# The odd feature's first operand: from four one-column products to a row of an existing product and a turn on VectorE

## The chip, the cores and the metric

The kernel runs on one core of a Trainium2 chip. The metric is the time of one execution on the device, in microseconds (us). The engines of the core are called by their short names in the profile: PE is TensorE, DVE is VectorE, ACT is ScalarE, POOL is GpSimd, and SP is the engine that issues most of the transfers. "PEld" is TensorE's loading of weights.

## What is computed

The input is x, 64 graphs of 256 nodes with 128 features, in float32, and one 256x256 matrix adj that all graphs share. Four layers follow each other, each with the form x = x + layer(max(layernorm(x), 0)), where the last one gives its result without the sum.

- Layer 0 is a gated recurrent unit over the graph, five steps of it.
- Layer 1 is a two-hop Chebyshev filter; layer 2 is a graph convolution with a normalised result.
- Layer 3 is an attention in which the score of every pair of nodes goes through a leaky ReLU feature by feature, and it is the bulk of the work:

```
s1 = einsum('bkf,ef->bke', x, W1)            # 256 features e for each node
s2 = einsum('bkf,ef->bke', x, W2)
pre = s1[:, :, None, :] + s2[:, None, :, :] + b_lin
h = where(pre >= 0, pre, 0.2 * pre)
e = einsum('bije,e->bij', h, a) + bias
out = sigmoid(einsum('bij,bjf->bif', softmax(e, axis=2), x))
```

In every layer the matrix that is called W or bias here is adj itself, so W1 and W2 are its two halves. For a pair of graphs, `pre` has 2 x 256 x 256 x 256 elements.

## The kernel before

The graphs are taken two at a time, so there are 32 pairs. The work on a pair has three parts.

The **front** of a pair (`front`, L483 to L731) does layers 0 to 2, the normalisation of layer 3 and the operands of the scores: it is a long chain of small products on PE with elementwise steps on ACT, DVE and POOL between them. A 512-column product with 128 features of output is written as four matmuls of 32 output columns each (`side_by_side`, L395), which stand side by side in the array. Transposes by PE (`to_feature`, `to_token`, L414 to L426) use the whole array.

The **tiles** of a pair are 64 slots. The leaky ReLU is split into a linear part and a clipped part. For the clipped part, a slot covers four nodes i of both graphs, and its 256 features lie in two halves on the partitions: a tile of 128 x 2048 elements is min(s1, s2) for one half. DVE makes a tile of the first half of the features with one instruction (L854), ACT makes one of the second half with eight (L868), and POOL makes some of either with eight (L876). In three slots of ten POOL makes the second half and adds it to DVE's tile with a transfer that accumulates (`add_pair`, L893), so that PE reads one tile there and not two. PE weighs the tiles with a by eight passes over 512 columns each (`score`, L935; a float32 matmul is two passes, and each of them has a record in the profile). There are 13 buffers for tiles, named `rl`.

The **tail** of a pair (`tail`, L733) is run once for each 128 of the 256 nodes. It adds the remaining parts to the scores, takes the softmax, weighs the nodes and stores the result.

The signs of a have to be sorted for this, so features with a positive factor stand first. Where the number of positive ones is odd, one feature is left over that belongs with neither half: the **odd feature**. It is not in the tiles. Its share of the score, min(s2o, s1o) with a value per node on each side, is added in the tail by one instruction for each graph (L739), which needs `s1o` with the nodes i on the partitions (128 x 4, for two graphs of two blocks of nodes) and `s2o` as a row of 512 nodes that is the same on all partitions. The linear part `lin` is such a row as well. The two rows come from one small product (L686): the weights `g2` are 32 columns, of which column 0 gives `lin` and column 1 gives `s2o`, and the others are zero. The four quarters of the 512 nodes go to partitions 0, 32, 64 and 96 of the result, ACT copies it to the tile `quarter` (L692), two transfers put rows 0 and 1 of each quarter into a row in memory (L699), and a third one spreads the row over all partitions (L702). The operand `s1o` comes from four more products that alternate with these (L688): here the activations are the weights, 128 x 128, and the moving operand is the single column `w1_odd`. ACT adds the bias and writes `s1o` (L694).

**The order of the work** is fixed when the program is built. A planner in the kernel holds a clock for each engine and a price for each step (`ran`, L106, with PROJECT, MIX, TURN and others, L448). Again and again it gives the engine whose clock stands lowest a step of a chain or a tile, takes the step that is ready, fronts and tails ahead of tiles, paces the front of the pair after next against the tiles that are weighed (`chain_ready`, L960), and gives POOL tiles of the other engines when it is ahead (`part_of`, L818). Every engine then runs its instructions in exactly that order, and each instruction waits for its data only. The planner's prices don't delay anything on the chip: they decide what stands where, and who makes which tile. Banks of PSUM for the front and the tail are taken from a list of three.

Of the kernel before, what the change touches and what calls it, by code (L numbers as in the profile page):

```python
# [8 lines left out]
F32 = mybir.dt.float32  # L9
AF = mybir.ActivationFunctionType  # L10
OP = mybir.AluOpType
# [3 lines left out]
P = 128  # L15
NB = 2
# [6 lines left out]
PE, DVE, ACT, POOL = ENGINES = (mybir.EngineType.PE, mybir.EngineType.DVE, mybir.EngineType.Activation, mybir.EngineType.Pool)  # L23
# [8 lines left out]
def kernel(  # L32
# [50 lines left out]
    nc = tc.nc  # L83
    B, N, D = x.shape
    NC = N // P
# [4 lines left out]
    const = ctx.enter_context(tc.tile_pool(name="const", bufs=1))  # L90
    work = ctx.enter_context(tc.tile_pool(name="work", bufs=2))
# [14 lines left out]
    def ran(engine, us, *after):  # L106
        start = max(clock[engine], 0.0, *after)
        if engine == ACT:
            behind[0] = max(0.0, behind[0] - (start - clock[ACT])) + 0.024 * us
        clock[engine] = start + us  # L110
        return clock[engine] + SEEN[engine] + (behind[0] if engine == ACT else 0.0)
# [6 lines left out]
    spare = [[b, 0.0] for b in banks[5:]]  # L118

    def take():  # L120

        spare.sort(key=lambda b: b[1])
        return spare.pop(0)
# [86 lines left out]
    win_n = const.tile([P, 63], F32, name="win_n")  # L210
    w1 = const.tile([P, N], F32, name="w1")
    w2n = const.tile([P, N], F32, name="w2n")
    odd_one = const.tile([P, 34], F32, name="odd_one")
    g2, w1_odd, b_odd = odd_one[:, 0:32], odd_one[:, 32:33], odd_one[:, 33:34]
    blin_s = const.tile([P, NE], F32, name="blin_s")
    SET_UP = set()

# [44 lines left out]
    def other_constants():  # L262
# [5 lines left out]
        t = ran(DVE, 0.8)  # L268

        for c in range(NC):  # L270
            yield PE, t, 1
            b = take()
            for k in range(NC):
                nc.tensor.matmul(b[0][:, 0:N], adj_t[:, k, c * P:(c + 1) * P], adj_n[:, k, :], start=(k == 0), stop=(k == NC - 1))
            t = ran(PE, 1.2, t, b[1])
            yield DVE, t
            nc.vector.tensor_scalar(adj_2[:, c, :], b[0][:, 0:N], 2.0, None, op0=OP.mult)
            t = ran(DVE, 0.35, t)
# [22 lines left out]
        t = ran(DVE, 1.5)  # L301
        yield PE, t, 1
        b = take()
# [5 lines left out]
        t = ran(PE, 0.6, t, b[1])  # L309
        yield DVE, t  # L310
        nc.vector.tensor_copy(columns(14, 3), b[0][:, 0:3])
        t = ran(DVE, 0.1, t)
# [27 lines left out]
        t = ran(DVE, 1.6)  # L340
# [11 lines left out]
        for c in range(NC):  # L352
            yield PE, t, 1
            b = take()
            for k in range(NE):
                nc.tensor.matmul(b[0][:, 0:N], adj_s[:, k, c * P:(c + 1) * P], moved_to[:, k].rearrange("p h m -> p (h m)"),
                                 start=(k == 0), stop=(k == NE - 1))
            t = ran(PE, 1.2, t, b[1])
# [5 lines left out]
            t = ran(DVE, 0.35, t)  # L364
# [3 lines left out]
        b = take()  # L368
# [8 lines left out]
        t = ran(PE, 1.4, t_in, b[1])  # L377
        yield DVE, t
        nc.vector.tensor_copy(blin_s, b[0][:, 1:4:2])
        nc.vector.tensor_copy(odd_one, b[0][:, 4:38])  # L380
        nc.vector.memset(win, 0.0)
        nc.vector.memset(win_n, 0.0)
        nc.vector.tensor_copy(win[:, 31:32], b[0][:, 0:1])
        nc.vector.tensor_scalar(win_n[:, 31:32], b[0][:, 0:1], -1.0, None, op0=OP.mult)
        t = ran(DVE, 0.7, t)
        spare.append([b[0], t])
        SET_UP.add("all")

# [11 lines left out]
    def flat(t):  # L400
        return t.rearrange("p b n -> p (b n)")
# [43 lines left out]
    SHORT = dict(tag="short", bufs=12)  # L445


    PROJECT, MIX, TURN, PRODUCT, PRODUCTS = 0.86, 1.74, 0.69, 0.88, 2.64  # L448
    COPY, BIASED, TANH, ELEMENTS = 0.48, 0.58, 0.57, 0.61

    def norm(src, since, h):
# [31 lines left out]
    def front(p):  # L483
# [8 lines left out]
        t = yield from norm(x0, 20.0 if p else 3.0, h)  # L492
        yield PE, t, 1
        b = take()
        to_feature(b[0], h)
        t_h = t
        t = ran(PE, TURN, t, b[1])
        yield ACT, t
        hT, t_hT = copied("hT", b, t)
        for step in range(STEPS):  # L500
            yield PE, t_h, 1, lambda: "adj" in SET_UP
            b = take()
            mix_nodes(b[0], h, adj_t)
            t = ran(PE, MIX, t_h, b[1])
            yield ACT, t
            mT, t_m = copied("mT", b, t)
            if p == 0:
# [6 lines left out]
                t = ran(PE, PROJECT, t_m)  # L514
# [3 lines left out]
            else:  # L518
# [4 lines left out]
                t = ran(PE, 2 * PROJECT, t_m, t_hT, pr[1])  # L523
# [3 lines left out]
            t = ran(ACT, TANH, t, r[1])  # L527
# [4 lines left out]
            if p == 0:  # L532
# [5 lines left out]
                t = ran(PE, PROJECT, t_rh)  # L538
            else:
# [7 lines left out]
                t = ran(PE, 2 * PROJECT, t_rh, pv[1])  # L547
# [6 lines left out]
            if p < 1:  # L554
                nc.scalar.activation(pv[0], pv[0], AF.Tanh, bias=bh, scale=1.0)
                t = ran(ACT, TANH, t)
                yield DVE, t
                nc.vector.tensor_sub(d, by_feature(pv[0]), hT)
                t = ran(DVE, ELEMENTS, t)
            else:  # L560
                nc.scalar.activation(d, by_feature(pv[0]), AF.Tanh, bias=bh, scale=1.0)  # L561
                t = ran(ACT, TANH, t)
# [3 lines left out]
                t = ran(POOL, 1.3, t)  # L566
            yield DVE, max(t, t_z)
            nc.vector.scalar_tensor_tensor(by_feature(pr[0]), by_feature(pr[0]), 1.0, d, op0=OP.add, op1=OP.mult)
            t = ran(DVE, ELEMENTS, t, t_z)
# [3 lines left out]
            hT = hT_new  # L573
            t_hT = ran(DVE, ELEMENTS)
# [3 lines left out]
            b = take()  # L578
            to_token(b[0], hT)
            t = ran(PE, TURN, t_hT, b[1])  # L580
# [9 lines left out]
        t = ran(DVE, ELEMENTS, t)  # L590
# [6 lines left out]
        b = take()  # L597
        mix_nodes(b[0], h, adj_n)
        t = ran(PE, MIX, t_h, b[1])
# [3 lines left out]
        b = take()  # L603
        to_feature(b[0], h)
        t = ran(PE, TURN, t_h, b[1])
        yield ACT, t
        hT, t = copied("hT", b, t)
        yield PE, t_h, 1
        b = take()
        mix_nodes(b[0], h, adj_2)  # L610
        t = ran(PE, MIX, t_h, b[1])
# [70 lines left out]
        t_s2a = ran(ACT, COPY, t_s2a)  # L682
        yield PE, t_hT, 1
        b = take()
        for g in range(4):
            nc.tensor.matmul(b[0][g * 32:(g + 1) * 32, 0:P], g2, flat(hT)[:, g * P:(g + 1) * P],  # L686
                             start=True, stop=True, skip_group_check=True)
            nc.tensor.matmul(b[0][:, P + g:P + g + 1], flat(hT)[:, g * P:(g + 1) * P], w1_odd, start=True, stop=True)  # L688
        t = ran(PE, 0.6, t_hT, b[1])
        yield ACT, t  # L690
        quarter = work.tile([P, P], F32, name="quarter", bufs=1)
        nc.scalar.copy(quarter, b[0][:, 0:P])  # L692
        s1o = work.tile([P, NB * NC], F32, name="s1o")
        nc.scalar.activation(s1o, b[0][:, P:P + NB * NC], AF.Identity, bias=b_odd, scale=1.0)  # L694
        t = ran(ACT, 0.35, t)
        spare.append([b[0], t])
        row = dram.tile([2, NB * N], F32, name="row", bufs=2)
        for k in range(2):
            nc.sync.dma_start(row[k].rearrange("(q n) -> q n", q=4), quarter[k:P:32, :])  # L699
            t = moved(t) if k else max(t, moved(t) - 2.2)  # L700
        rows = work.tile([P, 2, NB, N], F32, name="rows")
        nc.sync.dma_start(rows.rearrange("p k b n -> p (k b n)"), row.rearrange("k t -> (k t)").unsqueeze(0).to_broadcast([P, 2 * NB * N]))  # L702
# [352 lines left out]
```

## Time and profile before

| | |
|---|---|
| median of 3 runs | 4951.56 us (4950.31 to 4957.7) |
| time of the profiled execution | 4965.92 us |
| span of the profiled execution | 4964.1 us |
| instructions in the profile | 133991 |
| busy: PE, DVE, ACT, POOL | 4840.3, 4663.4, 4672.1, 4684.9 us |
| tiles: DVE L854, ACT L868, POOL L876 (instructions) | 1813, 10128, 8136 |

The profile is that of one execution, and its time is 14.4 us above the median of the runs. Its span leaves 1.8 us of its time outside. The busy time of PE is an upper figure, because matmuls overlap in its pipeline and their ends are modelled; the distance between the starts of two successive groups of matmuls tells better what one costs. A row of a table of groups gives the line, the engine, the operation, the tiles written and read, their shapes, the count, then the busy time in us and the mean duration in ns, and then the idle time of that engine just before. A row of the table of waits gives who waited for whom, the total in us, how often, and the longest.

### The profile page before, as it was taken

What the parts mean: (1) busy time and instruction counts of PE and PEld (TensorE: products, weight loads), DVE (VectorE), ACT (ScalarE), POOL (GpSimd) and SP (SyncE); (2) the same over time, 40 slices, a digit from 0 to 9 for tenths busy, and PEclk for the clock granted to TensorE, in tenths of its full rate; (3) what the DMA queues carried; (4) which work ended last, traced back from release to release, by engine and by line L of the source; (5) the groups of instructions that cost most, each with busy time, mean ns of one, the idle gap of its engine ahead of it and who ended that gap; (6) DMA issues with size and microseconds to landing.
All of it is one profiled execution on the core that took longest, in us unless ns stands there. A gap on an engine that the chain in (4) does not pass through costs nothing.

```text
span 4964.1 us, 133991 instructions
## 1 busy us (share of the span) xinstructions
PE 4840.3 (98%) x52487; PEld 1793.6 (36%) x52487; DVE 4663.4 (94%) x3288; ACT 4672.1 (94%) x12177; POOL 4684.9 (94%) x9454
## 2 busy tenths in 40 slices
PE   8999999999999999999999999999999999999987
PEld 3333333333333333333333333333333333333322
DVE  3899999999999999999999999999999999999998
ACT  3999999999999999999999999999999999999998
POOL 1899999999999999999999999999999999999998
PEclk9999999999999999999999999999999999999999
DMA  0577667667667676666776676767667767767677
GB/s 18 115 149 145 140 137 148 138 144 150 131 140 147 138 152 138 142 139 135 151 146 139 142 144 132 145 143 144 137 140 145 145 137 143 144 132 144 142 155 145
DMA packets 132363, 687.44 MB, mean 138 GB/s; under 512 B 14096, under 2 KB 49040, under 8 KB 53136
## 3 DMA queue, kind: packets, MB, share of 16 engines
q0 software_dynamic: 88416, 643.86, 64.7%
q1 hardware_dynamic: 42592, 35.01, 2.4%
q8 instruction: 410, 6.72, 0.5%
q14 instruction: 225, 1.84, 0.1%
q10 hardware_dynamic: 720, 0.00, 0.0%
HBM read 26.48 MB, written 8.52 MB: 7 GB/s over the span
## 4 chain that ended last, share of the span: by engine, by line
PE 58%; POOL 11%; DVE 8%; DMA 4%; ACT 4%; issue 3%; POOLq 0%; DVEq 0%; ACTq 0%
PE bank L935 36%; PE bank L398 18%; POOL rl L876 8%; DVE rl L854 6%; DMA rl<-rl 4%; ACT rl L868 3%; PE bank L426 2%; POOL rl L893 1%; PE bank L688 1%; PE bank L686 1%; PE bank L419 1%; POOL d L565 1%; DVE mv L464 0%; POOL mv L393 0%; DVE hT L572 0%
## 5 line engine op out<-in xcount | busy, mean ns | idle before, releaser
L854 DVE TENSOR_TENSOR rl<-s1a,bank 128x2048 f32<-128x2048 f32 x1813 | 4057.4, 2278 | 132.2 <-PE bank L935 70.2
L868 ACT ACTIVATE rl<-bank,s1b 128x256 f32<-128x256 f32 x10128 | 4045.6, 773 | 98.6 <-PE bank L935 57.6
L876 POOL TENSOR_SCALAR rl<-s2n,s1b 128x256 f32<-128x256 f32 x6256 | 2962.8, 669 | 65.0 <-PE bank L935 21.4
L935 PE MATMUL bank<-rl,win_n 128*32 128x512 f32 x17728 | 2198.3, 595 | 56.6 <-DVE rl L854 29.7
L935 PE MATMUL bank<-rl,win 128*32 128x512 f32 x10128 | 1322.4, 594 | 0.0
L935 PEld LDWEIGHTS bank<-rl,win_n 128*32 128x32 f32 x17728 | 555.1, 110 | 1220.6 <-issue 984.5
L876 POOL TENSOR_SCALAR rl<-s2c,s1a 128x256 f32<-128x256 f32 x1880 | 899.2, 658 | 13.6 <-PE bank L935 5.2
L893 POOL DMA_DIRECT2D rl<-rl x614 | 575.6, 949 | 12.5 <-DVE rl L854 6.8
L935 PEld LDWEIGHTS bank<-rl,win 128*32 128x32 f32 x10128 | 324.2, 110 | 653.4 <-issue 535.8
L398 PE MATMUL bank<-mT,wts 128*32 128x512 f32 x2560 | 337.3, 596 | 1.2 <-DVE rh L530 1.1
L398 PE MATMUL bank<-adj_t,h 128*32 128x256 f32 x5120 | 311.8, 383 | 4.8 <-ACT h L584 4.8
L565 POOL TENSOR_TENSOR d<-d,hT 128x512 f32<-128x512 f32 x155 | 227.3, 1466 | 70.0 <-ACT d L561 69.9
L398 PEld LDWEIGHTS bank<-adj_t,h 128*32 128x32 f32 x5120 | 167.8, 111 | 179.2 <-issue 62.1
L468 ACT ACTIVATE h<-x,mv 128x128 f32<-128x128 f32 x384 | 184.2, 766 | 17.3 <-DVE mv L464 16.9
L398 PE MATMUL bank<-hT,wts 128*32 128x512 f32 x1280 | 169.6, 597 | 0.0
L398 PE MATMUL bank<-mT,w 128*32 128x512 f32 x1280 | 168.4, 595 | 0.0
L398 PE MATMUL bank<-rh,u5t 128*32 128x512 f32 x1280 | 167.4, 592 | 0.0
L474 ACT COPY mT<-bank 128x512 f32<-128x512 f32 x160 | 130.4, 815 | 29.9 <-PE bank L398 25.2
L561 ACT ACTIVATE d<-bank,gate_b 128x512 f32<-128x512 f32 x155 | 146.4, 944 | 8.7 <-PE bank L398 8.6
L398 PEld LDWEIGHTS bank<-mT,wts 128*32 128x32 f32 x2560 | 83.5, 110 | 195.5 <-issue 150.8
L526 ACT ACTIVATE bank<-bank,gate_b 128x512 f32<-128x512 f32 x160 | 135.5, 847 | 18.8 <-PE bank L398 18.7
L549 ACT ACTIVATE bank<-bank,gate_b 128x512 f32<-128x512 f32 x160 | 144.2, 901 | 8.8 <-PE bank L398 8.5
(166 smaller groups left out, 3501.6 us busy)
## 6 DMA issues: line engine op xcount, KB each, us to landing
rl<-rl POOLq DMA_DIRECT2D x614, 1024.0 KB, 7.9
rows<-row SPq DMA_DIRECT2D x32, 512.0 KB
xin<-in_x_dram SPq DMA_DIRECT2D x64, 128.0 KB
out_dram<-o SPq DMA_DIRECT2D x64, 128.0 KB
row<-quarter SPq DMA_DIRECT2D x64, 2.0 KB
w_raw<-in_L_gnn_w_w_dram SPq DMA_DIRECT2D x3, 128.0 KB
th_raw<-in_L_gnn_Theta_dram SPq DMA_DIRECT2D x1, 320.0 KB
adj_n<-in_adj_dram SPq DMA_DIRECT2D x1, 256.0 KB
```

The source lines that it names most:

```text
L398: nc.tensor.matmul(o[g:g + 32], w[:, g:g + 32], t, start=start, stop=stop, skip_group_check=True)
L468: nc.scalar.activation(h[:, k, :], s[:, k, :], AF.Relu, bias=mv[:, k, 0:1], scale=mv[:, k, 1:2])
L474: nc.scalar.copy(c, by_feature(bank[0]))
L526: nc.scalar.activation(r[0], pr[0], AF.Tanh, bias=br, scale=0.5)
L549: nc.scalar.activation(pr[0], pr[0], AF.Tanh, bias=bz, scale=0.5)
L561: nc.scalar.activation(d, by_feature(pv[0]), AF.Tanh, bias=bh, scale=1.0)
L565: nc.gpsimd.tensor_sub(d, d, hT)
L854: nc.vector.tensor_tensor(t, rows.to_broadcast(whole), ops["s2a"].unsqueeze(1).to_broadcast(whole), op=OP.min)
L868: nc.scalar.activation(t[:, g, b, :], s2p[:, b, :], AF.Relu, bias=ops["s1"][1][:, b, i:i + 1], scale=-1.0)
L876: nc.gpsimd.tensor_scalar(t[:, part, b, :], ops["s2n" if k else "s2c"][:, b, :], ops["s1"][min(k, 1)][:, b, row], MOST_NEGATIVE, op0=OP.mi ...
L893: nc.gpsimd.dma_start(out=t.rearrange("p g b n -> p (g b n)"), in_=z.rearrange("p g b n -> p (g b n)"), accum_op=OP.add)
L935: nc.tensor.matmul(pe[g * 32:(g + 1) * 32, :], w[:, 31 - r:63 - r], flat(t[:, g]), start=False, stop=(left[block] == 0), skip_group_check= ...
```

## The change

The four one-column products and ACT's instruction on them are gone. Column 2 of the weights `g2`, which was zero, now holds the weights of the odd feature's first operand, so that row 2 of each quarter of the existing product is s1o without its bias, and nothing more is multiplied. To have it with the nodes on the partitions, DVE transposes the 128x128 tile `quarter` in its blocks of 32x32, and takes column 2 of each block, with the bias added, as `s1o`. For that to come out in the right places, the moving operand of matmul g is no longer the g-th quarter of the nodes, but the g-th 32 nodes of each block of 128; it is read with a stride. The two transfers of the rows put the nodes back in order: each moves 4 x 4 pieces of 32 elements, where it moved 4 pieces of 128. Two prices of the planner are changed with it and one is new, and so is one price that belongs to another step: TURN, for four transposes on PE.

```diff
-    odd_one = const.tile([P, 34], F32, name="odd_one")
-    g2, w1_odd, b_odd = odd_one[:, 0:32], odd_one[:, 32:33], odd_one[:, 33:34]
+    odd_one = const.tile([P, 33], F32, name="odd_one")
+    g2, b_odd = odd_one[:, 0:32], odd_one[:, 32:33]
...
-        nc.vector.tensor_copy(odd_one, b[0][:, 4:38])
+        nc.vector.tensor_copy(odd_one[:, 0:32], b[0][:, 4:36])
+        nc.vector.tensor_copy(odd_one[:, 2:3], b[0][:, 36:37])
+        nc.vector.tensor_copy(b_odd, b[0][:, 37:38])
...
-        t = ran(DVE, 0.7, t)
+        t = ran(DVE, 0.9, t)
...
-    PROJECT, MIX, TURN, PRODUCT, PRODUCTS = 0.86, 1.74, 0.69, 0.88, 2.64
+    PROJECT, MIX, TURN, PRODUCT, PRODUCTS = 0.86, 1.74, 0.80, 0.88, 2.64
...
+        tokens = flat(hT).rearrange("p (q g i) -> p q g i", g=4, i=32)
         for g in range(4):
-            nc.tensor.matmul(b[0][g * 32:(g + 1) * 32, 0:P], g2, flat(hT)[:, g * P:(g + 1) * P],
-                             start=True, stop=True, skip_group_check=True)
-            nc.tensor.matmul(b[0][:, P + g:P + g + 1], flat(hT)[:, g * P:(g + 1) * P], w1_odd, start=True, stop=True)
-        t = ran(PE, 0.6, t_hT, b[1])
+            nc.tensor.matmul(b[0][g * 32:(g + 1) * 32, 0:P], g2, tokens[:, :, g, :], start=True, stop=True, skip_group_check=True)
+        t = ran(PE, 0.35, t_hT, b[1])
         yield ACT, t
         quarter = work.tile([P, P], F32, name="quarter", bufs=1)
         nc.scalar.copy(quarter, b[0][:, 0:P])
+        t = ran(ACT, 0.3, t)
+        spare.append([b[0], t])
+        yield DVE, t
+        turned = work.tile([P, P], F32, name="turned", bufs=1)
+        nc.vector.transpose(turned, quarter)
         s1o = work.tile([P, NB * NC], F32, name="s1o")
-        nc.scalar.activation(s1o, b[0][:, P:P + NB * NC], AF.Identity, bias=b_odd, scale=1.0)
-        t = ran(ACT, 0.35, t)
-        spare.append([b[0], t])
+        nc.vector.tensor_scalar(s1o, turned[:, 2:P:32], b_odd, None, op0=OP.add)
+        ran(DVE, 0.4, t)
         row = dram.tile([2, NB * N], F32, name="row", bufs=2)
         for k in range(2):
-            nc.sync.dma_start(row[k].rearrange("(q n) -> q n", q=4), quarter[k:P:32, :])
+            nc.sync.dma_start(row[k].rearrange("(q g i) -> g q i", g=4, i=32), quarter[k:P:32, :].rearrange("g (q i) -> g q i", i=32))
```

Lines of the changed kernel stand 2 further on from L383 on and 5 further on after this place, so L854 becomes L859, L868 becomes L873, L876 becomes L881 and L935 becomes L940. The new matmuls are L689, the transpose L698 and the addition L700.

## The prediction

> **What bounds the kernel now.** I read the busy shares on the page first, then stretches of the span, then PE's timeline around the lines that change, then the waits.
>
> ```profile
> PE 4840.3 (98%) x52487; PEld 1793.6 (36%) x52487; DVE 4663.4 (94%) x3288; ACT 4672.1 (94%) x12177; POOL 4684.9 (94%) x9454
> ```
>
> Four engines stand close together, so the average decides nothing. Busy time by stretch (length, then PE, PEld, DVE, ACT, POOL) says more:
>
> ```profile
> 0.00:134.90 134.90, 111.94 (x1103) 49.75 (x1107) 42.77 (x116) 46.60 (x82) 14.84 (x26) 0.87 0.07 18
> 134.90:4940.00 4805.10, 4716.97 (x51300) 1740.12 (x51294) 4615.73 (x3165) 4623.21 (x12090) 4669.22 (x9427) 1.00 0.70 142
> 4940.00:4964.10 24.10, 11.35 (x95) 3.71 (x94) 4.86 (x8) 2.30 (x6) 0.88 (x1) 0.71 0.40 82
> ```
> ```profile
> 2000.00:3000.00 1000.00, 988.86 (x10796) 365.00 (x10792) 956.46 (x665) 956.54 (x2495) 974.76 (x1967) 1.00 0.69 142
> ...
> 4800.00:4940.00 140.00, 118.55 (x1062) 33.61 (x1058) 138.81 (x71) 139.94 (x383) 139.37 (x291) 0.99 0.78 159
> ```
>
> The first tile starts at 134.9, and the last 24 us are one pair's tail. Between them, with fronts in the mix, PE is 99% busy while DVE and ACT idle 4% and POOL 2.5%. After the last front (4800 on) it is the reverse: PE 85%, the others above 99%. So the three elementwise engines can run full when PE has room, and in the steady stretch they don't.
>
> PE's timeline over one occurrence of the changed lines:
>
> ```profile
> 2501.53 1.04 PE L935 MATMUL bank<-rl,win_n 128*32 128x512 f32 x8
> 2502.38 0.38 PE L686 MATMUL bank<-hT,odd_one 128*32 128x128 f32 x2
> 2502.70 0.38 PE L688 MATMUL bank<-odd_one,hT 128*128 128x1 f32 x2
> 2503.01 0.41 PE L686 MATMUL bank<-hT,odd_one 128*32 128x128 f32 x2
> ...
> 2504.64 0.38 PE L688 MATMUL bank<-odd_one,hT 128*128 128x1 f32 x2
> 2504.95 1.06 PE L935 MATMUL bank<-rl,win 128*32 128x512 f32 x8
> ```
>
> From 2502.38 to 2504.95 is 2.57 us, back to back, while eight 512-column passes of L935 take 0.85. The narrow products and the full-array ones alternate, so neither kind overlaps with itself. The same distance is 2.57 us in 31 of the 32 fronts and 4.32 in the first, at half clock: 84.0 us in all.
>
> Waits in 500 to 4500 us (total, times, longest):
>
> ```profile
> DVE rl L854 <- PE bank L935: 58.7, 97, 2.0
> ACT rl L868 <- PE bank L935: 51.7, 71, 2.7
> ...
> DVE rl L854 <- DMA rl<-rl: 35.2, 27, 3.7
> ACT rl L868 <- DMA rl<-rl: 31.1, 22, 3.4
> ...
> POOL rl L876 <- PE bank L935: 22.7, 27, 2.4
> ```
>
> The largest waits of all three are for tile buffers that PE hasn't weighed yet. PE paces the steady stretch, though by little.
>
> **What the Trainium skill says.** "TensorEngine Tiling (Array Packing)", section Key Properties: different column tiles can load and multiply in parallel, while a change of tiling mode drains TensorE. The trace agrees: four 32-column matmuls with 128 moving columns (th_raw and w,yT rows) start four in 109 ns, but each of the eight parts here takes 0.31 to 0.33 us. "Perfetto Trace Analysis", section Identifying the Most-Contended Engine, says that matmul busy time is no good measure for TensorE; so I count distances between starts. "VectorE: DVE Perf Modes", section The three transpose paths, prices VectorE's transpose of 128x128 at 311 ns in bf16, in 32x32 blocks; no run here shows it.
>
> **The change part by part.**
>
> *PE.* 84.0 us go. In come four side-by-side matmuls of two passes, 2 x 0.109 = 0.22 us per front, 7 us in 32. The net is 77 us: 2.35 in each later front, about 3.9 in the first (4.32 less twice 0.22). The strided moving operand has no precedent in the trace. Its runs are 32 contiguous elements; nothing to gain from it, and if it halved the rate, 0.22 us per front, 7 us in all. I take no extra.
>
> *ACT.* 32 instructions of L694 go, 10.9 us. The planner gives it 24 fewer tile instructions (10104), at 4045.6/10128 = 0.40 us: 9.6. Together 20.5 less.
>
> *DVE.* 32 transposes and 32 additions on 128x4 come. For the transpose the nearest rows are elementwise instructions on 128x128 (L297, 285 ns); with the skill's 311, I take 0.30, with 0.28 and 0.55 (if four bytes halve the rate) as ends. For the addition, 0.17 (L258, 128x2), at most 0.37 (L464, 128x4). That is 0.47 us per pair, 15 us (14 to 29). It also gets 4 more tiles (1817) at 4057.4/1813 = 2.24: 9.0. Together 24 more. The copies at set-up (two more, 0.16 each) lie before 134.9, where DVE is two thirds idle; without that cover, 0.3 us.
>
> *POOL.* 8 fewer instructions (8128) at 0.475: 3.8 less.
>
> *Waits.* The transpose waits for ACT's copy of `quarter`; behind it in DVE's queue stand tile instructions (L854 before, L859 now) or the step L568, for whom PE waits. The addition waits for the transpose, a few tenths inside the 0.47. The bank comes free an ACT instruction (0.34) sooner. s1o and the rows are used 90 us later (first rows issued 133.2, first L739 at 223.5), so neither DVE's step nor slower landing of shorter pieces reaches anything: 64 transfers, 0.5 us each on SP; were issue twice as long, 32 us on an SP that has 240 transfers in the whole span. Without the 90 us it would be the landing, which the trace doesn't give; up to a microsecond or two per pair.
>
> *The planner.* Its price of the odd step was 0.6 where 2.57 was spent. Four transposes cost about 0.70 (in PE's timeline the passes begun at 2489.74 last to 2490.60, and the group after the transposes starts at 2491.30); their price goes from 0.69 to 0.80, ten times per pair. Per pair the plan was 2 us short on PE; now it's some 1 us over. No price delays anything; it moves the order towards PE being early, which should cut waits, but I count nothing for it.
>
> **The sum**, on the profiled execution. Start: 134.9 - 3.9 = 131.0. End: 24.1. The middle is the longest of:
>
> - PE: 30 of its fronts' steps lie in the stretch that PE paces (234.8 to 4628.8; the last is at 4781.7): 4805.1 - 30 x 2.35 = 4734.6. Span 4889.7.
> - POOL: 4669.2 - 3.8 = 4665.4 busy, 54 us of short gaps between its instructions (under 0.1 us each), and longer waits, now 82. In the table above those for PE and the accumulating transfers (15.9) are 38.6 of 71.5, so 44 of the 82; I let PE's share (26) go and two thirds of the transfers' (18): 44 stay. Middle 4763, span 4918.
> - DVE: 4615.7 + 24 = 4639.7 busy, waits now 189. For PE (58.7 + 13.4 on the tail's reciprocal) they're 44%, for the transfers 21%; with the same cuts 80 stay, and 5 new: middle 4725, span 4880.
> - ACT: 4623.2 - 20.5 = 4602.7 and even all of its 182: 4785. With the same cuts below DVE.
>
> So POOL becomes the bound, at 4918; with 1.8 outside the span 4920 against 4965.9, 46 us less. The same 46 off the median of 4951.56 gives **4906 us**.
>
> **The rivals.**
>
> *All of it comes through.* PE keeps the pace with as little slack as now, and POOL's waits shrink with it. For it: POOL's short waits may largely be PE's delay passed through the transfers; in 4800 to 4940 it was busy 99.5%. Against it: at a middle of 4735, POOL would have 16 us for all its long waits. Span 4890: median 4877.
>
> *Little comes through.* The order is new from the first pairs on, and the three engines' waits for each other (DVE for POOL's L393 and L565, POOL for DVE, the transfers) stay as they are. If half of POOL's 26 for PE goes and nothing else, 69 of its 82 stay: middle 4788, span 4944, 20 less; median 4931.
>
> *Slower: DVE's queue behind the new wait.* One instruction on DVE now waits for ACT in every front, and ACT already runs late at times (DVE L530 waited for ACT 25.8 us in 13 cases, the longest 6.9). While DVE stands, tiles of 2.24 us each stand behind it and PE runs dry. DVE's busy and its waits that aren't PE's make 4639.7 + 106 = 4746 in the middle; it passes the old 4805 once the new wait averages above (4805 + 4 - 4746)/32 = 2.0 us. At 3 us the middle is 4842, the span 4997, the median 4984. Against it: the planner puts the transpose after the copy by its clock, and behind one to three tile instructions that cover lateness.
>
> *It doesn't shorten PE's step:* the strided operand makes the four run one after another. At 0.27 us per pass (L686's alone takes that long), eight take 2.2 us and 0.4 of 2.57 is saved, 13 us of PE in all, with DVE's 24 us in its idle time: at most 13 us, median near 4942.
>
> **How the numbers follow.** A measurement of this kernel tells about 0.2% (9.9 us) from no change. The likeliest case, 4890 to 4925: 0.57. All comes through, 4865 to 4890: 0.14. Little comes through, 4925 to 4941: 0.14. Within 0.2%, the serial matmuls or a new order that eats the rest: 0.06. Slower: 0.09. So faster 0.85. The range of 8 in 10 goes from 4872 to 4943; it leaves about 0.05 below and 0.15 above, and DVE's upper bound (14 us more) and the stride's 7 lie within it.
>
> **What would show it.** In the profile after: matmuls on `quarter`'s bank from 0.2 to 0.3 us apart from the next group, not 2.57; the first tile near 131; transposes near 0.3 us; DVE's and ACT's waits for PE's L940 well below 58.7 and 51.7 in the same stretch; POOL's share of the middle above 98%; PE's below 98.5%. It is wrong if the transpose waits above 2 us on average, if PE stays at 99% with a shorter step (then something else fills it), or if POOL's long waits don't fall.

## The result and the profile after

The changed kernel takes 4942.76 us (median of 20 runs), the kernel before 4952.4 us in 20 runs: a ratio of 0.9978, 95% interval 0.9971 to 0.9984. It is faster by some 10 us. The forecast was 46 us faster, 4906; the direction was right and the size was not. The profile after shows a run at its kernel's median. The profile of before stands 14 us above its own; the first experiment tells why.

The changed step itself became what the sum made of it. PE's timeline of the changed kernel (start, time to the modelled end, engine, line) around one occurrence:

```profile
2485.62 0.40 PE L689 MATMUL bank<-hT,odd_one 128*32 128x128 f32 x8
2485.84 1.04 PE L940 MATMUL bank<-rl,win 128*32 128x512 f32 x8
```

The next group starts 0.22 us later. Summed over the 32 fronts the distances are 7.2 us, where they were 84.0: PE's 77 us are gone, and the strided operand costs nothing that can be seen (eight passes start within 0.22 us, as the sum had it). The span of the profiled execution is 4940.7 us (its time is 4942.5), and the busy line and two stretches (as before: length, then PE, PEld, DVE, ACT, POOL) read:

```profile
PE 4758.5 (96%) x52231; PEld 1739.0 (35%) x52231; DVE 4682.1 (95%) x3358; ACT 4644.4 (94%) x12121; POOL 4659.6 (94%) x9446
```
```profile
2000.00:3000.00 1000.00, 977.43 (x10764) 355.28 (x10756) 964.01 (x678) 960.09 (x2512) 968.67 (x1962) 1.00 0.69 141
...
4800.00:4920.00 120.00, 97.85 (x911) 28.71 (x907) 117.79 (x61) 120.00 (x331) 117.03 (x243) 0.99 0.80 161
```

PE is down from 989 to 977 in that thousand, and DVE, ACT and POOL stand at 96 to 97% as they did. So PE got room, and no other engine filled up. The waits in 500 to 4500 us of the changed kernel say what they wait for now:

```profile
PEld bank L428 <- DVE hT L574: 108.0, 79, 3.2
ACT rl L873 <- DMA rl<-rl: 66.0, 39, 5.2
...
DVE rl L859 <- DMA rl<-rl: 57.1, 50, 3.5
...
PE bank L428 <- DVE hT L574: 48.4, 54, 2.6
...
ACT rl L873 <- PE bank L940: 44.4, 50, 4.1
...
POOL rl L881 <- DMA rl<-rl: 26.7, 26, 2.5
...
DVE rl L859 <- PE bank L940: 13.0, 30, 2.1
...
POOL rl L881 <- PE bank L940: 7.9, 11, 2.2
```

DVE's and POOL's waits for PE fell from 58.7 to 13.0 and from 22.7 to 7.9, as forecast; ACT's hardly did (51.7 to 44.4). But the waits for the accumulating transfers, which the sum let fall by two thirds, rose: for DVE from 35.2 to 57.1, for ACT from 31.1 to 66.0, for POOL from 15.9 to 26.7. And PE, early now, stands before its transposes until DVE has made hT: 156 us (PE and its weight loads) where it was 75. Two theories could account for a gain of 10 us instead of 46. **A**: the gain was lost in the new order of the instructions, which the planner's changed prices made. **B**: behind PE there was at once another bound, whatever the order.

### The profile page after: what moved, and what is told of

Read it like the earlier page. It is cut to its first block, busy times and chain, and to the rows that moved or that the text cites. A ratio compares the mean times of both kernels' runs of the same rounds, so it can differ in the third digit from the quotient of the medians.

```text
span 4940.7 us, 133662 instructions
## 1 busy us (share of the span) xinstructions
PE 4758.5 (96%) x52231; PEld 1739.0 (35%) x52231; DVE 4682.1 (95%) x3358; ACT 4644.4 (94%) x12121; POOL 4659.6 (94%) x9446
## 5 line engine op out<-in xcount | busy, mean ns | idle before, releaser
L873 ACT ACTIVATE rl<-bank,s1b 128x256 f32<-128x256 f32 x10104 | 4050.2, 793 | 128.9 <-DMA rl<-rl 70.9
L859 DVE TENSOR_TENSOR rl<-s1a,bank 128x2048 f32<-128x2048 f32 x1817 | 4064.8, 2280 | 90.4 <-DMA rl<-rl 62.7
L881 POOL TENSOR_SCALAR rl<-s2n,s1b 128x256 f32<-128x256 f32 x6280 | 2951.1, 656 | 64.2 <-DMA rl<-rl 28.2
L940 PE MATMUL bank<-rl,win_n 128*32 128x512 f32 x17752 | 2191.5, 594 | 57.1 <-DVE rl L859 28.9
L940 PE MATMUL bank<-rl,win 128*32 128x512 f32 x10104 | 1316.5, 594 | 0.0
L940 PEld LDWEIGHTS bank<-rl,win_n 128*32 128x32 f32 x17752 | 559.4, 110 | 1216.5 <-issue 992.8
L881 POOL TENSOR_SCALAR rl<-s2c,s1a 128x256 f32<-128x256 f32 x1848 | 872.7, 637 | 5.9 <-DMA rl<-rl 1.2
L940 PEld LDWEIGHTS bank<-rl,win 128*32 128x32 f32 x10104 | 323.1, 110 | 641.4 <-issue 533.1
L428 PE MATMUL bank<-ident,hT 128*128 128x128 f32 x640 | 105.4, 288 | 69.2 <-DVE hT L574 61.7
L528 ACT ACTIVATE bank<-bank,gate_b 128x512 f32<-128x512 f32 x160 | 144.3, 902 | 20.5 <-PE bank L400 16.5
L551 ACT ACTIVATE bank<-bank,gate_b 128x512 f32<-128x512 f32 x160 | 151.4, 946 | 11.3 <-PE bank L400 11.3
## 6 DMA issues: line engine op xcount, KB each, us to landing
rl<-rl POOLq DMA_DIRECT2D x614, 1024.0 KB, 7.9
```

The costliest lines, as they stand in the source:

```text
L528: nc.scalar.activation(r[0], pr[0], AF.Tanh, bias=br, scale=0.5)
L551: nc.scalar.activation(pr[0], pr[0], AF.Tanh, bias=bz, scale=0.5)
L859: nc.vector.tensor_tensor(t, rows.to_broadcast(whole), ops["s2a"].unsqueeze(1).to_broadcast(whole), op=OP.min)
L873: nc.scalar.activation(t[:, g, b, :], s2p[:, b, :], AF.Relu, bias=ops["s1"][1][:, b, i:i + 1], scale=-1.0)
L881: nc.gpsimd.tensor_scalar(t[:, part, b, :], ops["s2n" if k else "s2c"][:, b, :], ops["s1"][min(k, 1)][:, b, row], MOST_NEGATIVE, op0=OP.mi ...
L940: nc.tensor.matmul(pe[g * 32:(g + 1) * 32, :], w[:, 31 - r:63 - r], flat(t[:, g]), start=False, stop=(left[block] == 0), skip_group_check= ...
```

## The experiments

Each run is told as its ratio to the kernel before on the same chip, since the level of that kernel differed between occasions: its median was 4952 to 4955 us on three chips and in the 20 runs above, and 4965 and 4967 us on two other chips. A gain in us in what follows is the ratio's distance from 1, times 4952.

### The same order, only PE's step shortened

```diff
-            nc.tensor.matmul(b[0][:, P + g:P + g + 1], flat(hT)[:, g * P:(g + 1) * P], w1_odd, start=True, stop=True)
...
-        nc.scalar.activation(s1o, b[0][:, P:P + NB * NC], AF.Identity, bias=b_odd, scale=1.0)
+        nc.scalar.activation(s1o, b[0][:, 0:NB * NC], AF.Identity, bias=b_odd, scale=1.0)
```

> The kernel before with only the four one-column products (L688) taken out; s1o is then made from other columns of the same bank, so the odd feature's part of the score is not the reference's. The planner's prices are as before, and every engine's order of instructions is that of before. PE's step shrinks from 2.57 to 0.22 us per front and DVE gets nothing. Theory A, the gain was lost in the new order: 4900 to 4917, since PE's freed time comes through where the order is the old one. Theory B, PE was only just ahead of the next bound, which is the engines' waits for each other and for the accumulating transfers whatever the order: 4932 to 4945, with the waits of DVE, ACT and POOL for PE falling and those for transfers rising by about as much.

Measured: 0.9939 (0.9926 to 0.9952), 30 us. That is between the two theories' figures, so each holds a part: even in the old order only two fifths of the 77 us come through, and the whole change brought a third of these 30. Its waits in 500 to 4500 us:

```profile
PEld bank L426 <- DVE hT L572: 92.1, 71, 3.2
...
DVE rl L853 <- DMA rl<-rl: 49.5, 39, 3.1
...
ACT rl L867 <- PE bank L934: 44.3, 59, 3.0
...
ACT rl L867 <- DMA rl<-rl: 34.5, 27, 3.5
...
DVE rl L853 <- PE bank L934: 28.1, 50, 2.2
...
POOL rl L875 <- DMA rl<-rl: 17.9, 21, 2.6
...
POOL rl L875 <- PE bank L934: 9.1, 8, 2.4
```

With the order untouched, the waits for PE fall and those for transfers don't: over the four engines these are 138 us, where they were 103. They aren't PE's lateness passed on, or they would have fallen with it.

The busy line of this run, and its middle from the first tile to the last tail (length, then PE, PEld, DVE, ACT, POOL), can be set beside the prediction's sum for POOL:

```profile
PE 4769.6 (97%) x52231; PEld 1746.9 (36%) x52231; DVE 4654.2 (95%) x3288; ACT 4665.8 (95%) x12177; POOL 4664.9 (95%) x9454
```
```profile
133.10:4897.70 4764.60, 4649.71 (x51058) 1695.35 (x51054) 4606.73 (x3165) 4617.32 (x12090) 4649.15 (x9427) 1.00 0.70 143
```

POOL has the same 9454 instructions in the same order as in the profile of before, and they take 20 us less, 4664.9 instead of 4684.9. That is the occasion, not the edit. Where POOL's tile instructions follow each other directly, one starts 451 ns after the other in the profile of before and 449 ns here. For tiles of whole width it is 451 in every profile from the two chips with the level of 4965 and 4967, and 449 in every other one. So the profile from which the sum was made belongs, by POOL's pace, to the slower kind of occasion, and the medians of the result to the faster. With a level that is 11 to 12 us higher on the chips of the slower pace, that accounts for most of the 14 us between them.

POOL is idle for 115 us of this middle. Gaps under 0.1 us make 54 of them, as the sum took it. The longer waits were 82 us and are 62; the sum let them fall to 44. An estimate for the occasion of the profile of before: 0.9939 of its span is 4934 us, and with this run's start and end, POOL's 4669 us of that occasion and 54 of short gaps, 55 us of longer waits are left, give or take 6.

### The whole change in the old order

The changed kernel with the planner's prices of before, and DVE's two instructions not charged.

> The whole change, but with the planner's prices of before (TURN 0.69, odd step 0.6, nothing charged for DVE's two new instructions, which stand in DVE's order where ACT's step was planned). All other instructions stand in the order of before. Theory A: 4903 to 4922, well below the changed kernel's 4943. Theory B: 4935 to 4950, the same as the changed kernel within 0.2%. A third outcome, above 4952, would say that the two instructions on DVE cost their price and more, through waits for ACT's copy.

Measured: 0.9967 (0.9954 to 0.9979). That is in theory B's range, 0.0028 above the run before it, 14 us. The two runs differ in DVE's two instructions, which stand where nobody planned them: they take 1.56 us per front from the transpose to the next instruction, and 0.89 in the changed kernel, where the plan has them; and the transpose made DVE wait for ACT's copy 11 times, 12.7 us in all. They also differ in ACT's instruction that is gone and in the shorter pieces of the row transfers. That DVE's part makes the 14 us is likely and not shown.

### TURN by itself

```diff
-    PROJECT, MIX, TURN, PRODUCT, PRODUCTS = 0.86, 1.74, 0.80, 0.88, 2.64
+    PROJECT, MIX, TURN, PRODUCT, PRODUCTS = 0.86, 1.74, 0.69, 0.88, 2.64
```

> The changed kernel with TURN at 0.69 instead of 0.80, nothing else; a new order results. Theory A in the form that the overcharge of TURN spoils the order: 4905 to 4928. Theory B: 4935 to 4950. If orders are a lottery of some 10 to 20 us whatever the prices, anything from 4925 to 4960, with PE idle in the same places as in the changed kernel.

> The kernel before with TURN at 0.80 and nothing else changed. Theory A (the price of TURN makes a worse order): 4965 to 4990. Theory B: 4945 to 4962, no change that can be measured, since PE is full in either order.

> The changed kernel with TURN at 0.74, between 0.69 (0.9954 of before) and 0.80 (0.9978); 0.60 gave 1.0003. If the price acts by itself: 0.995 to 0.998, and PE's waits for ACT's h between 62 and 103 us. If orders are drawn by chance: anywhere in 0.992 to 1.002.

> The changed kernel with TURN at 0.60, below what four transposes cost (0.70). With 0.80 ACT's copy of h came 1.06 us after the transposes on average and PE waited 103 us for h in 500 to 4500 us, with 0.69 0.87 and 62. If a price above the cost is what does harm, since ACT is given one more piece of a tile before the copy: 0.994 to 0.997 of before, as with 0.69. If lower is better still: below 0.994. If prices only draw another order out of many: anywhere in 0.993 to 1.000, and waits for h not in step with the price.

Measured: the change with 0.69 gives 0.9954 (0.9943 to 0.9966); the kernel before with 0.80 gives 1.0033 (1.0021 to 1.0045); the change with 0.74 gives 0.9972 (0.9962 to 0.9983), with 0.60 it gives 1.0003 (0.9994 to 1.0011). The first of these lies just above theory A's range, the second within it. So the new price costs 0.0024 in the changed kernel and 0.0033 in the kernel before, 12 and 16 us, though nothing waits for a price. In both, PE's waits for ACT's tiles h grew by the same amount: 59 to 101 us in the kernel before, 62 to 103 in the changed one (500 to 4500 us). In these pairs ACT's copy of hT after the transposes also starts later, 1.65 us after them on average instead of 1.35 in the kernel before, 1.70 instead of 1.29 in the changed one. That fits a plan which takes the transposes to end later and gives ACT a piece of a tile first, which no run shows by itself. But neither the waits nor the time follow the price. At 0.74 the waits for h are 110 us, longer than at 0.80, while the ratio lies between those of 0.69 and 0.80. At 0.60 they are shortest (47 us) and the time is worst; there PE waits 75 us for transfers and 88 for DVE's tiles. So the 12 and 16 us are what two pairs of orders differ by, and not a cost per unit of the price; that any price would draw a better or a worse order by chance isn't ruled out.

### DVE's new addition

The changed kernel's own rows show that the addition of four columns is dear (what the expectations call the port is the idea that DVE and POOL share a way into SBUF; the last section comes back to it):

```profile
L698 DVE STREAM_TRANSPOSE turned<-quarter x32: 289/306/314, 127.3 to 4755.8; 128x128 f32<-128x128 f32 x32
L700 DVE TENSOR_SCALAR s1o<-turned,odd_one x32: 229/392/2326, 127.7 to 4756.2; 128x4 f32<-128x4 f32 x32
```

The three numbers are the shortest, median and longest duration in ns. The edit takes it out, and ACT adds the bias in its copy:

```diff
-        nc.scalar.copy(quarter, b[0][:, 0:P])
+        nc.scalar.activation(quarter, b[0][:, 0:P], AF.Identity, bias=b_rows, scale=1.0)
...
-        nc.vector.tensor_scalar(s1o, turned[:, 2:P:32], b_odd, None, op0=OP.add)
+        s1o = turned[:, 2:P:32]
```

> The changed kernel without DVE's addition: the bias goes into ACT's copy of the product (a bias per partition that is zero outside rows 2, 34, 66 and 98), and the tail reads the turned tile. Every other instruction stands where the changed kernel has it. Theory of the port: DVE's addition takes 0.23 us where POOL is idle and up to 2.3 us where POOL's instructions stand close[...]; without it DVE gains 0.55 us per front on average, 18 us in all, and 5 to 10 us of them come through: 4932 to 4939. Rival: the addition's waits fall into time in which DVE would have waited anyway: 4940 to 4946.

> The same removal of the addition in the kernel with TURN at 0.69, where the addition took 0.99 us on average (to 4.3), so 32 us of DVE. Theory of the port: 10 to 20 us faster than with the addition, 4912 to 4922. Rival: 4928 to 4934, no change.

Measured: 0.9983 (0.9977 to 0.9989) beside the changed kernel's 0.9978, and 0.9947 (0.9935 to 0.9959) beside 0.9954. The first is its rival's figure; the second lies between its two expectations, and its interval covers no change. So nothing that could be measured changed in either. The addition's long durations are real, and taking them out brings no time. With the share of DVE's time that comes through in the next experiment (0.13), 18 us would have brought 2 to 3 us, which these intervals can't tell from nothing.

### How much of each engine's time comes through

In these the orders are those of before, and one engine's tiles are a little narrower, for instance POOL's:

```diff
+CUT = 8
...
-                nc.gpsimd.tensor_scalar(t[:, part, b, :], ops["s2n" if k else "s2c"][:, b, :], ops["s1"][min(k, 1)][:, b, row],
+                nc.gpsimd.tensor_scalar(t[:, part, b, 0:N - CUT], ops["s2n" if k else "s2c"][:, b, 0:N - CUT], ops["s1"][min(k, 1)][:, b, row],
```

> The kernel before, every engine's order unchanged, with POOL's tile instructions 248 columns wide instead of 256 (8 of every 256 columns of its tiles are left out). That takes some 11 ns from each of 8136, about 90 us from POOL's busy time. Theory C, the four engines are coupled and none of them alone sets the pace: a fifth to a third comes through, 4925 to 4936, like the 28 us that came of PE's 77. Theory D, POOL was the bound behind PE: over half, below 4908.

> The kernel before, orders unchanged, with DVE's tile instructions 250 columns wide instead of 256 (6 of every 256 columns of its tiles are left out): [...]50 ns from each of 1813, about 90 us of DVE. Theory C: 4925 to 4940. Theory D in the form that DVE is the bound behind PE, since PE waited longest for DVE's hT in the changed kernel: below 4908.

> The kernel before, orders unchanged, with ACT's tile instructions 244 columns wide instead of 256 (12 of every 256 columns of its tiles are left out), some 8 ns from each of 10128, about 85 us of ACT. Taken from PE, POOL and DVE in the same order, 77, 52 and 84 us of busy time brought 28 to 30, 26 to 28 and 11 us: shares of 0.38, 0.5 and 0.13, which already make up 1. Theory C, the pace is shared and the shares add to one: ACT's share is near nothing, 0 to 10 us faster than before. Rival: the shares don't add up to anything and ACT brings 20 us or more as well.

> The kernel before, orders unchanged, with the four one-column products taken out (the odd feature's part of the score is then not the reference's) and POOL's tile instructions 248 columns wide (8 of every 256 columns of its tiles are left out). Alone these brought about 0.6% and 0.5%. If the engines hold each other up in turn, the two together bring at least their sum: 0.985 to 0.989 of before. If POOL becomes the bound once PE is relieved, as the prediction had it, more than the sum: below 0.985. If a third bound stands close behind both (DVE, ACT, the transfers), less: above 0.991.

The busy lines of the three with one engine cut (POOL, DVE, ACT) show by how much:

```profile
PE 4838.3 (98%) x52487; PEld 1792.9 (36%) x52487; DVE 4662.3 (94%) x3288; ACT 4671.2 (94%) x12177; POOL 4632.8 (94%) x9467
```
```profile
PE 4841.2 (98%) x52487; PEld 1797.4 (36%) x52487; DVE 4579.3 (92%) x3288; ACT 4671.1 (94%) x12177; POOL 4685.2 (95%) x9467
```
```profile
PE 4836.7 (98%) x52487; PEld 1792.9 (36%) x52487; DVE 4662.2 (94%) x3288; ACT 4576.2 (92%) x12177; POOL 4665.5 (94%) x9467
```

| taken from | us taken | ratio | us gained | share |
|---|---|---|---|---|
| PE | 77 | 0.9939 (0.9926 to 0.9952) | 30 | 0.39 |
| POOL | 52 | 0.9947 (0.9935 to 0.9959) | 26 | 0.50 |
| DVE | 84 | 0.9978 (0.9970 to 0.9987) | 11 | 0.13 |
| ACT | 88 to 96 | 0.9993 (0.9986 to 0.9999) | 3 | 0.04 |
| PE and POOL | 77 and 53 | 0.9847 (0.9834 to 0.9861) | 76 | |

What was taken is counted between profiles with the same pace of POOL: the first two lines above are from a chip where POOL's tile instructions of whole width start 451 ns apart, as in the profile of before. The third, like the run with PE and POOL cut, is from one with 449; its POOL has 4665.5 us although only ACT's work was cut. (In two other profiles from that chip ACT's tile instructions start 357.0 ns apart instead of 357.8; hence the range in its row.)

POOL's cut was smaller than expected (6 to 7 ns from each instruction, not 11), and its share, a half, lies between those of the two theories. Together PE and POOL bring more than their sum of 56: once PE is relieved, POOL's 53 us bring 46, with an interval of some 9 us to either side. So POOL is close behind PE, as the prediction's sum had it; the run's figure itself stands on the border between the two expectations of at least the sum and more than the sum. DVE and ACT hardly matter. That the four shares add to about 1 is no rule, since PE's and POOL's don't add up when both are cut.

### The accumulating transfers

```diff
-        nc.gpsimd.dma_start(out=t.rearrange("p g b n -> p (g b n)"), in_=z.rearrange("p g b n -> p (g b n)"), accum_op=OP.add)
+        nc.gpsimd.dma_start(out=t[:, 0:2].rearrange("p g b n -> p (g b n)"), in_=z[:, 0:2].rearrange("p g b n -> p (g b n)"), accum_op=OP.add)
```

> The kernel before, orders unchanged, with each accumulating transfer moving half of the tile (the other half of POOL's part is left out of the sum). The transfers land some 2 to 3 us sooner than 7.9. If waits for the transfers are a bound of their own behind PE (they were 31 to 66 us per engine in the changed kernel), 15 to 40 us faster than before. Theory C without the transfers: up to 10 us faster.

> The changed kernel with accumulating transfers of half the size (half of POOL's part is left out of the sum), orders unchanged. In the kernel before the same cut brought 46 us. Theory L: PE's freed time is waiting behind the transfers, so here the cut brings clearly more than 46 us from the changed kernel's 0.9978, to 0.980 to 0.986 of before. Rival, it brings the same 46 or less, since the changed order loses elsewhere (PE's waits for ACT's h): 0.987 to 0.992.

The transfers of the first of these (size, and median us from issue to landing), where the kernel before has 1024.0 KB and 7.9:

```profile
rl<-rl POOLq DMA_DIRECT2D x614, 512.0 KB, 4.8
```

Measured: 0.9906 (0.9892 to 0.9919) in the kernel before, 46 us with no engine's work cut, more than either theory had, and 0.9866 (0.9853 to 0.9879) in the changed one, 55 us from its 0.9978. In both the waits of DVE, ACT and POOL for transfers go to under 4 us each, and PE's to nothing. So the time to the transfers' landing was a bound beside PE in the kernel before already, at 98% busy PE. The second result lies between the figures of its two theories, and the difference of 9 us between the two gains isn't clear of noise: that the change made the transfers a heavier bound isn't shown, and most of the 55 us was there before.

### The plan's price of a landing

The planner takes a transfer to land 6.6 us after the end of its issue. In the traces it is 6.9 (median), and over 10.7 in one of twenty. So some buffers and tiles are planned for moments at which they aren't there.

```diff
-ISSUE, ADDED, LANDED, SLACK = 0.65, 5.3, 6.6, 0.3
+ISSUE, ADDED, LANDED, SLACK = 0.65, 5.3, 7.9, 0.3
```

> The changed kernel with TURN at 0.69 and the planner's price for the landing of an accumulating transfer raised from 6.6 to 7.9 us; it really takes 6.9 (median) from the end of the issue, 10.7 for one in twenty. A new order results. Theory L, what holds the kernel back with PE relieved is that PE and the tile buffers wait for transfers that the plan expects too early: 0.988 to 0.993 of before, and waits for transfers below those with 6.6. Rival: an order as good or bad as any other, 0.994 to 1.000.

> The kernel before with the landing price at 7.9 instead of 6.6 and nothing else. If the better price of a landing is what brought 31 of the 42 us of the run with TURN at 0.69, and PE didn't bound the kernel before: 0.990 to 0.995 of before. If PE's 77 us more of work keep the kernel before from using it: 0.996 to 1.001.

> The changed kernel as it is, TURN at 0.80, with the landing price at 7.9. If waits for transfers are what took the gain and the plan's price of them sets these waits, 0.990 to 0.9945 of before, with waits for transfers in 500 to 4500 us below 80 us over the four engines (168 in the changed kernel). If TURN's effect stays beside it: 0.002 or more above the run with TURN at 0.69 (0.9915). If the 0.9915 was the luck of one order: 0.995 to 1.000.

| program | landing 6.6 | landing 7.9 |
|---|---|---|
| before | 1 | 0.9965 (0.9951 to 0.9979) |
| changed, TURN 0.80 | 0.9978 (0.9971 to 0.9984) | 0.9933 (0.9920 to 0.9945) |
| changed, TURN 0.69 | 0.9954 (0.9943 to 0.9966) | 0.9915 (0.9902 to 0.9927) |

The waits for transfers in the last of these, 500 to 4500 us:

```profile
POOL rl L881 <- DMA rl<-rl: 12.8, 7, 4.5
...
ACT rl L873 <- DMA rl<-rl: 10.4, 7, 2.2
...
DVE rl L859 <- DMA rl<-rl: 8.9, 6, 3.0
```

The table is nearly additive. In each row the landing price brings 0.0035 to 0.0045, and the waits for transfers over the four engines fall from 103 to 21, from 168 to 41 and from 111 to 43 us. That is a new order in each case too, but three pairs of orders agree. For the kernel before, the figure falls among those of its second expectation, that PE's extra work keeps it from using the better price; but the changed kernel gains no more, so that isn't the reason. In each column the change with TURN at 0.69 brings 0.0046 to 0.0050, and TURN at 0.80 takes 0.0018 to 0.0024 of it back (at 7.9 the two intervals overlap). At the price of 7.9 the waits for h are the same at both TURNs (44 and 45 us), so what TURN costs there, if anything, is not those waits, and stays open. The kernel with TURN 0.69 and landing 7.9, 4910 us, beats both kernels of this study by more than the change did.

### Fewer joined slots

> The changed kernel with TURN at 0.69 and 28 slots in a hundred joined by a transfer instead of 30: some 41 tiles go from POOL to ACT, with 41 transfers of 614 fewer, and PE weighs 41 tiles more (35 us). Theory: PE has room now, POOL and the transfers have not, ACT has: 0.988 to 0.993 of before. Rival: PE is still the bound and the order is another: 0.996 to 1.003.

Measured: 0.9973 (0.9962 to 0.9984), with an interval that overlaps that of the same kernel with 30 in a hundred (0.9954). The edit didn't do what the expectation says. The transfers went from 614 to 573 and PE weighs 41 tiles more, but the planner gave the work back to POOL: its tile instructions rose from 8112 to 8192 (ten tiles of eight), ACT's fell from 10064 to 10056, and DVE made 9 tiles fewer. So this run says nothing on taking work from POOL.

## Why the prediction was right or wrong

**PE's step, and that the stride costs nothing:** right, 2.57 to 0.22 us.

**DVE's 0.47 us per front, ends 14 and 29 us in all:** the transpose was right (0.31). The two together took 0.89 us per front, 28 us: the value taken was wrong, and the upper bound held in this order, though not in the one with TURN at 0.69 (42 us) or the old one (50 us). That DVE has the time for it was right in the sense that removing the addition brings nothing. The whole of DVE's new step with the order that comes with it, TURN aside, is the difference between 0.9939 and 0.9954, 7 us where the sum had none; the two intervals overlap.

**The step that failed first: POOL's waits.** "I let PE's share (26) go and two thirds of the transfers' (18): 44 stay." With only PE's step shortened and every order as before, 62 of the 82 us stay (by the estimate, 55 in the occasion of the profile), so 20 to 27 us of waits go where the sum took 38. In 500 to 4500 us, 9.1 of POOL's 22.7 us for PE stay, and its 15.9 for the transfers become 17.9. Those waits have a cause beside PE's lateness, as the half-size transfers and the landing price show. PE's relief is worth 30 us and not 46. Of these 16 us some 11 are the waits, by the same estimate; 4 are the eight instructions of POOL that only the new plan takes from it, and 2 are the first tile, which came at 133.1 us and not at 131.0 (in the changed kernel it comes at 131.2). In the changed kernel the waits for transfers rose from 103 to 168 us over the four engines. POOL's longer waits are 89 us there and its share of the middle is 97.0%, where the prediction named more than 98% and a fall of these waits as its signs.

**"So POOL becomes the bound, at 4918":** POOL's time then comes through almost in full, so that it stands next is right, with the transfers beside it. The span is right by luck: 4920.3 was profiled with only PE's step shortened, but in a faster occasion. There POOL is busy for 4649 us of the middle where the sum has 4665, and idle for 115 where it has 98 (54 and 44), and the two differences cancel. "The same 46 off the median" was a fair step; what it took off was too much.

**"No price delays anything ... I count nothing for it": wrong.** The first half is true. But the order that TURN 0.80 makes costs 12 us in the changed kernel and 16 in the kernel before.

So of the forecast 46 us, 16 are lost in what PE's relief brings, POOL's waits above all, 7 in DVE's step and its order, and 12 by TURN, which leaves 11, and 10 was measured. These are the steps from one run to the next, so they add up by themselves; a different way through the runs would give each another size. Of the rivals, "little comes through" is nearest. It kept the waits for transfers, and left 69 of POOL's 82 us; 62 were measured in the old order. It had neither the 7 us nor TURN's 12. DVE's queue behind the transpose, the slower rival, didn't come: in the changed kernel the transpose made DVE wait once, 5.7 us in the first front.

## What to carry to other kernels

In a kernel with several engines near 95%, a busy share can't tell who sets the pace: shorten one engine at a time by a per cent with the order fixed, and see what share comes through. Here it was 0.39 of PE's time, 0.50 of POOL's, 0.13 of DVE's and next to nothing of ACT's, and the time to a transfer's landing weighed as much as PE did: half-size transfers brought 46 us.

Before two spans are compared, look at one instruction that the edit doesn't touch. Here POOL's same instructions took 4685 us in some profiles and 4665 in others, and a forecast span seemed to be met because of it. And a wait that is put down to one engine doesn't all go when that engine is relieved: 9.1 of POOL's 22.7 us for PE stayed here. Where an order is planned from prices, a changed price is an edit with a cost of its own; take it apart from the edit that it came with.

## What the runs showed that was not expected

POOL has two paces. Its tile instructions start 451 ns apart in the profiles from two chips and in the profile of before, and 449 ns apart in those from three other chips and in that of the changed kernel. It makes 20 us in the busy time of the same instructions (4685.2 and 4665.5 in two runs above, 4659.6 in the changed kernel and 4679.8 in it without DVE's addition), and goes with a level of the whole kernel that is 11 to 12 us higher. What sets the pace is not shown.

DVE's addition on 128x4 elements takes 0.23 us at the least, as in the first front, where POOL does nothing, and up to 2.3 us (4.3 with TURN at 0.69, 6.1 in the old order) where POOL's instructions follow each other closely. Of the 30 that took over 0.5 us in these three kernels, 24 ended within 0.08 us of the end of a POOL instruction; the longest of them sat through a dozen POOL instructions, so the end of one isn't enough. The transpose just before it stays between 0.289 and 0.314 us whatever POOL does. The Trainium skill, "GPSIMD Engine Reference", section Specifications, says that POOL shares SBUF interfaces with VectorE, with contention for VectorE's instructions in a two-port mode or with two SBUF inputs; these durations fit that, though no run here shows in which mode the addition runs or takes the mode away by itself.
